# The last half piece of an expert's second weights: loaded a step ahead into a place of its own and copied by ScalarE

## The chip, the core and the metric

The kernel runs on one core of a Trainium2 chip. The metric is the device time of one execution in microseconds. Three runs of the kernel before gave 1069.84, 1070.74 and 1071.74 us; the median is 1070.74 us.

## What is computed

The input is a graph of 625 nodes with 768 features and 20,000 edges. A two-layer graph attention network is added to the normalised nodes, then a transformer block of one layer (causal attention with 12 heads and a mixture of 8 experts) is added to the result. The change touches only the mixture, which in the reference is:

```python
h2 = _ln(x, ln2_g, ln2_b).reshape(-1, d)          # 625 x 768
w, sel = jax.lax.top_k(h2 @ Wg, 1)                 # one expert per row
w = jax.nn.softmax(w, axis=-1)                     # of one value: 1
combine = zeros((n, 8)).at[arange(n)[:, None], sel].add(w)
hid = jax.nn.relu(jnp.einsum('nd,edf->enf', h2, W1) + b1[:, None, :])   # 3072 hidden
y = jnp.einsum('enf,efd->end', hid, W2) + b2[:, None, :]
moe = jnp.einsum('ne,end->nd', combine, y)
```

Each row needs only the expert that its gate chose. The weights of one expert are W1 (768 x 3072) and W2 (3072 x 768) in float32, 18.9 MB together.

## The kernel before

The graph layers and the attention fill the first 620 us or so and are not touched. The mixture works on rows sorted by expert in DRAM (`xg` holds the normalised rows, `xr` the sums so far with the row's number). Rows of one expert are cut into blocks of 128, 64 or 32 rows. A first block of 128 rows, of the expert that most rows of the first tile chose, is worked on ahead of the loop while the rest is still being sorted (`step_a`, line 1179). All other blocks are steps of one hardware loop (line 1333). A table made on the chip (lines 1264 to 1306) gives for every step its expert (row 0), whether this expert is new or the same as in the step before (row 1), the kind of the block (row 2) and its first row (row 3). In this input the loop has nine steps.

**The weights in SBUF.** There is one set of buffers for one expert: `w1[c]` and `w2[c]`, c = 0 to 2, each for 1024 of the 3072 hidden features. Each of the six pieces is loaded as two halves of 1536 KB (`load_piece`, lines 1028 to 1040; the issues are lines 1037 for W1 and 1031 for W2). The piece that this change is about is the second half of `w2[2]`, the last one in the order.

**A step** (`step`, line 1075) multiplies the block's rows with W1 in chunks (`into`, line 1091), copies the sums with VectorE (line 1095), turns them with TensorE (`turn`, line 1102), applies bias and ReLU with ScalarE (line 1107), and multiplies with W2 (`out_of`, line 1114) into `py`, which gathers over all chunks. In between it turns the next block's rows (`turn_rows`, lines 891 and 892). At its end VectorE adds `py` to the row sums (line 1166) and GpSimd scatters the rows to the output (line 1168). Blocks of 64 and 32 rows are laid side by side in the array, 2 or 4 at a time; there each `out_of` reads a whole `w2[c]`. The code of a step exists three times in the loop, one for each kind, behind `tc.If`.

**The order of the loads.** `load_expert(e, new)` (line 1066) comes after a step's own work (`all_of`, line 1325) and issues the loads for the *next* step: W1 in six halves, the bias row, W2 in six halves. SyncE issues them in exactly this order. Each waits until TensorE has read the buffer that it overwrites for the last time in this step, so the loads follow TensorE's reading through the step; the very last half can be issued only at the step's end. If the next step has the same expert, the issues are still executed by SyncE, with their waits, but move nothing (the condition `new`). `next_expert(i + 1)` (line 1319) reads the expert and the flag of the next step from the table into SyncE's registers at the start of a step.

Ahead of the loop the first expert's weights are loaded without a condition (lines 1051, 1052 and 1312), and one `load_expert` for the loop's step 0 follows `step_a` (line 1323). The loop is entered by every engine for itself: each adds an offset to the semaphores that it is responsible for, SyncE after it has read the number of steps (line 1331).

Of the kernel before, what the change touches and what calls it, by code (L numbers as in the profile page):

```python
# [9 lines left out]
F32 = mybir.dt.float32  # L10
F16 = mybir.dt.float16
BF16 = mybir.dt.bfloat16
I32 = mybir.dt.int32
# [11 lines left out]
D = 768  # L25
# [17 lines left out]
NS = E * 2 + N // B  # L43
# [4 lines left out]
FC = 1024  # L48
NFC = DF // FC
# [13 lines left out]
def gnn_moe_kernel(ctx: ExitStack, tc: tile.TileContext, p, out):  # L63
    nc = tc.nc
# [3 lines left out]
    keep = ctx.enter_context(tc.tile_pool(name="keep", bufs=1))  # L68
# [70 lines left out]
    def load_vector(b, v):  # L139
        nc.gpsimd.dma_start(b, row_bcast(v, D))  # L140
        return b[:R]
# [5 lines left out]
    with tc.tile_pool(name="gnn", bufs=1) as gp:  # L147
# [31 lines left out]
        with tc.tile_pool(name="oneh", bufs=12) as op_, \  # L179
# [20 lines left out]
            ahead = flat.bitcast(I32)[:G, GE:]  # L200
# [27 lines left out]
            def step(at, on_act):  # L228
                o = op_.tile([R, SH + 1], F16, name="step")
                if on_act:  # L230
                    nc.scalar.activation(o, iota[:, :SH + 1], AF.Sign, bias=at, scale=-1.0)  # L231
                else:
                    nc.vector.tensor_scalar(o, iota[:, :SH + 1], at, 2.0, op0=OP.is_lt, op1=OP.mult)
                return o
# [232 lines left out]

        sx = ctx.enter_context(tc.tile_pool(name="sx", bufs=1, side="right", reuse_waits="tile"))  # L470
        l1g = load_vector(sx.tile([B, D], F32, tag="xa", name="l1g"), p["L0_ffn_ln1_g"])
        l1b = load_vector(sx.tile([B, D + 1], F32, tag="ra", name="l1b")[:, :D], p["L0_ffn_ln1_b"])
        norms = keep.tile([R, T, 4], F32, name="norms")
        with tc.tile_pool(name="gw", bufs=2, reuse_waits="tile") as gw, \
# [68 lines left out]
            w2 = halves("w2", p["L0_gnn_W2"], KH, D)  # L543
# [138 lines left out]

    pos = [keep.tile([R, 1], I32, name=f"pos{t}") for t in range(T)]
    nblk = keep.tile([1, 1], I32, name="nblk")
    table = keep.tile([1, 4, NS + 1], I32, name="table")
    first = keep.tile([1, 1], I32, name="first")
    sxt = ctx.enter_context(tc.tile_pool(name="sxt", bufs=1, side="right", reuse_waits="tile"))
    xaT = sxt.tile([128, KD, B], F32, name="xaT")
    pool, SP, PE = mybir.EngineType.Pool, mybir.EngineType.SP, mybir.EngineType.PE
    rt = ctx.enter_context(ExitStack())  # L690
    ap = rt.enter_context(tc.tile_pool(name="rt", bufs=1, side="right", reuse_waits="tile"))
    with tc.tile_pool(name="att", bufs=1, reuse_waits="tile") as a1, \
# [107 lines left out]
        def queries_keys(j):  # L800

            i, c0 = j // 3, (j % 3) * 128
            qk[j] = [aw.tile([128, N], F32, name=n, bufs=2) for n in ("qT", "kT")]
            for dst, w, scale in ((qk[j][0], wq[i], D ** -0.5), (qk[j][1], wk[i], 1.0)):
                for a, b in ((0, SH), (SH, N)):
                    pp = ps.tile([128, 512], F32, tag="p1", name="pq")
                    for c in range(KD):
                        nc.tensor.matmul(pp[:, :b - a], w[:, c, c0:c0 + 128], hT[:, c, a:b],  # L808
                                         start=(c == 0), stop=(c == KD - 1))
                    nc.scalar.activation(dst[:, a:b], pp[:, :b - a], AF.Copy, scale=scale)  # L810
                    yield
# [172 lines left out]
        ahead = iter(())  # L984
        for i in range(len(units) + 2):
            if i < len(units):
                j, t = units[i]
                if t == 0:
                    for _ in ahead:
                        pass  # L990
                    ahead = queries_keys(j + 1) if j < last else iter(())
# [29 lines left out]
    W1, W2, b2 = p["L0_ffn_W1"], p["L0_ffn_W2"], p["L0_ffn_b2"]  # L1021
    w1, w2 = [None] * NFC, [None] * NFC

    def piece(ew, l, c):
        (w2 if l else w1)[c] = ew.tile([128, FC // 128, D] if l else [128, KD, FC], F32,
                                       name=f"ew{l}_{c}")

    def load_piece(e, l, c, **cond):
        if l:
            for k in range(0, FC // 128, 4):  # L1030
                nc.sync.dma_start(  # L1031
                    w2[c][:, k:k + 4, :],
                    W2[ds(e, 1), c * FC + k * 128:c * FC + (k + 4) * 128, :]
                    .rearrange("o (k p) d -> p (o k) d", p=128), **cond)
        else:
            for k in range(0, KD, 3):
                nc.sync.dma_start(
                    w1[c][:, k:k + 3, :],
                    W1[ds(e, 1), k * 128:(k + 3) * 128, c * FC:(c + 1) * FC]
                    .rearrange("o (k p) f -> p (o k) f", p=128), **cond)  # L1040

    def load_bias(e, **cond):
        nc.sync.dma_start(b2b, b2[ds(e, 1), :].to_broadcast([B, D]), **cond)
# [5 lines left out]
    piece(ewa, 0, 0)  # L1049
    piece(ewa, 1, 0)  # L1050
    load_piece(first_e, 0, 0)
    load_piece(first_e, 1, 0)
    b2b = mw.tile([B, D], F32, name="b2b", bufs=1)
    load_bias(first_e)

    def sums_so_far(row):
        rb = mw.tile([B, D + 1], F32, name="rb", bufs=1)
        nc.gpsimd.dma_start(rb, xr[ds(row, B), :])
        return rb

    def biases(e):
        bT = mw.tile([128, NK], F32, name="bT")
        of_e = bT_all.rearrange("p (e k) -> p e k", k=NK)[:, ds(e, 1), :]
        return bT, nc.vector.tensor_copy(bT, of_e.rearrange("p o k -> p (o k)"))

    def load_expert(e, new):

        with tc.manual_schedule(engines={SP}):
            for l in range(2):
                for c in range(NFC):  # L1070
                    load_piece(e, l, c, cond=new)
                if not l:
                    load_bias(e, cond=new)

    def step(M, xT, bT, rb, after=None):

# [120 lines left out]
    def row8(name, *shape, tag=None):  # L1197
        return ap.tile([1, *shape], F32, name=name, tag=tag or name)
# [67 lines left out]
    ioe = iota("ioe", [[0, NS], [1, E]], NS, E)  # L1266
    sel = row8("sel", NS, E)
    v.tensor_tensor(sel, inc[:, None, :].to_broadcast([1, NS, E]), ios, op=OP.is_le)
    tabf = row8("tabf", 4, NS + 1)
    v.memset(tabf, 0.0)  # L1270
    who = row8("who", NS)
    v.tensor_reduce(who, sel, AX.X, OP.add)
# [42 lines left out]
    row_0 = nc.values_load(table[0:1, 3, 0:1], engines=[pool], min_val=0, max_val=NR - B)  # L1315
    first_rows = nc.gpsimd.dma_start(xb, xg[ds(row_0, B), :])
    first_turned, = step_a

    def next_expert(i):
        return (nc.values_load(table[0:1, 0, ds(i, 1)], engines=[SP], min_val=0, max_val=E - 1),  # L1320
                nc.values_load(table[0:1, 1, ds(i, 1)], engines=[SP], min_val=0, max_val=1))

    load_expert(*next_expert(0))

    def all_of(step, e, new):
        with tc.manual_schedule(engines={PE}):
            for _ in step:
                pass
        load_expert(e, new)

    n_blk = nc.values_load(nblk[0:1, 0:1], min_val=1, max_val=NS)
    sp_order.close()
    with tc.For_i(0, n_blk, 1, iteration_sync="reg_based") as i:  # L1333
        e = nc.values_load(table[0:1, 0, ds(i, 1)], engines=[mybir.EngineType.DVE], min_val=0,
                           max_val=E - 1)
        kind = nc.values_load(table[0:1, 2, ds(i, 1)], min_val=0, max_val=2)
        row, row_next = (nc.values_load(table[0:1, 3, ds(k, 1)], engines=[pool], min_val=0,
                                        max_val=NR - B) for k in (i, i + 1))

        nc.gpsimd.dma_start(xb, xg[ds(row_next, B), :])  # L1340
        rb = sums_so_far(row)
        bT, s = biases(e)
        tc.add_manual_dep(s.ins, first_rows.ins.name, ORDER)

        then = next_expert(i + 1)
        with tc.If(kind == 0) as cmp:
            all_of(step(B, xbT, bT, rb, first_turned), *then)
        with cmp.Else():
            with tc.If(kind == 1) as cmp2:
                all_of(step(64, xbT, bT, rb, first_turned), *then)  # L1350
            with cmp2.Else():
                all_of(step(32, xbT, bT, rb, first_turned), *then)
# [31 lines left out]
```

## Time and profile before

| | us |
|---|---|
| median of 3 runs | 1070.74 |
| the profiled execution, its own time | 1070.6 |
| its span in the profile | 1067.9 |
| first block's work ahead of the loop | 627.9 to 698.8 |
| loop, TensorE from first to last matmul | 700.1 to 1055.2 |

The granted TensorE clock over the span is 0.985. In the page, engines are named PE (TensorE matmul), PEld (its weight loads), DVE (VectorE), ACT (ScalarE), POOL (GpSimd) and SP (SyncE); a "q" behind a name means the engine's instruction queue, so SPq L1031 is SyncE issuing the loads of line 1031. A group's line gives the engine, the operation, output and input, the count, then busy time and mean duration, then the engine's idle time just ahead of the group and what ended most of it. In the loop the steps begin, by TensorE's first matmul, at 700.13, 736.35, 801.68, 840.54, 866.12, 931.47, 965.72, 993.27 and 1027.52 us.

### The profile page before, as it was taken

How to read it: one execution, taken by the hardware profiler on the slowest of the kernel's cores; microseconds unless marked ns; L12 is line 12 of the kernel's file. 1: busy time of each engine (PE TensorE's matmuls, PEld its weight loads, DVE VectorE, ACT ScalarE, POOL GpSimd, SP SyncE). 2: the span in 40 equal slices, each digit the busy share in tenths (PEclk: the TensorE clock that was granted, in tenths of full speed). 3: DMA queues.
4: the chain of work that ended last, by engine and by line, in shares of the span. 5: the costliest groups of instructions: out<-in, count | busy, mean ns of one | idle time of the engine just before them, and what ended most of it. 6: DMA issues, size and time to landing. Idle time of an engine off the chain costs nothing. (4 is left out here: it accounts for less than half of the span.)

```text
span 1067.9 us, 14435 instructions
## 1 busy us (share of the span) xinstructions
PE 1006.7 (94%) x4763; PEld 574.8 (54%) x4764; DVE 451.7 (42%) x1264; ACT 319.0 (30%) x817; POOL 57.1 (5%) x97
## 2 busy tenths in 40 slices
PE   6889999999999999999999999999999889998993
PEld 4455465677656556666665654544453435533341
DVE  6886786484284910665438544011101121011211
ACT  6677553452231111444435211110202112021120
POOL 1200100000000100000001101000000000000000
PEclk9999999999999999999999999999999899998997
DMA  9300500301300347998002679012799948899693
GB/s 286 129 1 1 181 9 0 133 1 43 93 14 0 103 120 220 398 389 293 1 2 63 237 251 351 12 46 58 304 321 387 408 177 322 294 413 409 248 412 153
DMA packets 85669, 194.48 MB, mean 182 GB/s; under 512 B 32397, under 2 KB 34068, under 8 KB 85609
## 3 DMA queue, kind: packets, MB, share of 16 engines
q1 hardware_dynamic: 79817, 174.00, 44.3%
q0 software_dynamic: 5712, 19.54, 5.3%
q8 instruction: 36, 0.59, 0.2%
q10 hardware_dynamic: 80, 0.16, 0.1%
q14 instruction: 24, 0.20, 0.1%
HBM read 251.98 MB, written 38.37 MB: 272 GB/s over the span
## 5 line engine op out<-in xcount | busy, mean ns | idle before, releaser
L1114 PE MATMUL py<-ew,hbT 128*64 128x384 f32 (+2 forms) x960 | 196.0, 517 | 12.8 <-DMA ew<-in_L_ffn_W_dram 12.8
L1091 PE MATMUL ph<-ew,xbT 128*32 128x256 f32 (+2 forms) x864 | 153.9, 499 | 7.8 <-issue 4.5
L1114 PEld LDWEIGHTS py<-ew,hbT 128*64 128x64 f32 (+2 forms) x960 | 91.6, 149 | 97.7 <-issue 62.3
L1107 ACT ACTIVATE hbT<-tph,bT 128x64 f32<-128x64 f32 (+2 forms) x240 | 55.3, 333 | 264.2 <-PE tph L1102 162.3
L1091 PEld LDWEIGHTS ph<-ew,xbT 128*32 128x32 f32 (+2 forms) x864 | 63.9, 135 | 87.2 <-issue 79.9
L1166 DVE TENSOR_TENSOR yo<-yo,py 64x384 f32<-64x384 f32 (+2 forms) x40 | 23.0, 608 | 182.9 <-PE py L1114 182.5
L1095 DVE COPY hb<-ph 128x512 f32<-128x512 f32 (+1 forms) x39 | 24.5, 629 | 149.8 <-PE ph L1091 149.8
L528 PE MATMUL agg<-xl,zT 125*125 125x256 f32 (+1 forms) x300 | 79.8, 417 | 1.3 <-ACT zT L517 1.1
L528 PEld LDWEIGHTS agg<-xl,zT 125*125 125x125 f32 x300 | 54.5, 188 | 19.6 <-ACT zT L517 2.6
L231 ACT ACTIVATE step<-iota,past 125x314 f16<-125x314 f16 x120 | 55.9, 548 | 0.0
L356 PE MATMUL pp<-w,yT 128*125 128x512 f32 x120 | 55.3, 600 | 0.0
L628 PE MATMUL ph<-wr,h1T 128*125 128x384 f32 x160 | 52.8, 486 | 0.0
L590 PE MATMUL ph<-w,h1T 128*125 128x384 f32 x160 | 52.4, 486 | 0.0
L837 ACT ACTIVATE e<-e,nm 125x125 f32<-125x125 f32 (+4 forms) x60 | 36.0, 602 | 39.5 <-DVE nm L834 39.5
L248 PE MATMUL cps<-step,oh 125*125 125x314 f16 x181 | 37.4, 309 | 10.5 <-ACT step L231 5.4
L900 PE MATMUL po<-wpj,aT 128*125 128x384 f32 x120 | 44.3, 499 | 1.2 <-DVE nm L834 0.7
L241 DVE TENSOR_SCALAR oh<-iota,drel,upper 125x125 f16<-125x125 f16 x160 | 41.2, 317 | 3.4 <-PE cps L248 3.4
L166 PE MATMUL ph<-wr,yT 128*125 128x512 f32 x96 | 42.1, 593 | 0.1
L590 PEld LDWEIGHTS ph<-w,h1T 128*125 128x125 f32 x160 | 30.0, 188 | 21.2 <-issue 0.5
L628 PEld LDWEIGHTS ph<-wr,h1T 128*125 128x125 f32 x160 | 29.8, 187 | 20.8
L808 PE MATMUL pq<-hT,L_ffn_Wq 128*128 128x313 f32 (+1 forms) x144 | 40.9, 432 | 0.0
L834 DVE CUSTOM_DVE_ANT_0 e<-sc,later 125x125 f32<-125x125 f32 (+4 forms) x60 | 30.7, 544 | 24.1 <-PE sc L828 23.9
(328 smaller groups left out, 1248.9 us busy)
## 6 DMA issues: line engine op xcount, KB each, us to landing
ew<-in_L_ffn_W_dram SPq DMA_DIRECT2D x132, 1536.0 KB
xr<-zt SPq DMA_DIRECT2D x5, 3076.0 KB
xg<-zt SPq DMA_DIRECT2D x5, 3072.0 KB
w<-in_L_gnn_W_dram SPq DMA_DIRECT2D x4, 1536.0 KB
wr<-in_L_gnn_Wr_dram SPq DMA_DIRECT2D x4, 1536.0 KB
b2b<-in_L_ffn_b_dram SPq DMA_DIRECT2D x11, 384.0 KB
xb<-xg POOLq DMA_DIRECT2D x10, 384.0 KB, 6.1
rb<-xr POOLq DMA_DIRECT2D x9, 384.5 KB, 7.0
```

Of the source, the lines that this page charges most:

```text
L166: nc.tensor.matmul(pp[:R, :], yT[:, c, cols(t)], part(wr1, KD, c, i, 512), start=(c == 0), stop=(c == KD - 1))
L231: nc.scalar.activation(o, iota[:, :SH + 1], AF.Sign, bias=at, scale=-1.0)
L241: m = nc.vector.tensor_scalar(o, iota[:, :n], at, weight, op0=OP.is_equal, op1=OP.mult)
L356: nc.tensor.matmul(pp[:R, :], yT[:, c, cols(t)], part(w1, KD, c, i, 512), start=(c == 0), stop=(c == KD - 1))
L528: nc.tensor.matmul(self.agg[:R, c0:c0 + n], zT[:, s, :], xl[:, s, x0:x0 + n], start=(s == 0), stop=(s == T - 1))
L590: nc.tensor.matmul(ph[:R, :384], h1T[:, c, cols(t)], part(w2, KH, c, i, 384), start=(c == 0), stop=(c == KH - 1))
L628: nc.tensor.matmul(ph[:R, :384], h1T[:, k, cols(t)], part(wr2, KH, k, i, 384), start=(k == 0), stop=(k == KH - 1))
L808: nc.tensor.matmul(pp[:, :b - a], w[:, c, c0:c0 + 128], hT[:, c, a:b], start=(c == 0), stop=(c == KD - 1))
L900: mm = nc.tensor.matmul(pp[:R, i, :384], aT[:, c, cols(t)], wpj[i][:, c, :], start=(c == 0), stop=(c == KD - 1))
L1091: mm = nc.tensor.matmul(ph[g * M:(g + 1) * M, :C], xT[:, k, :M], w[:, k, o + g * C:o + (g + 1) * C], start=(k == 0), stop=(k == KD - 1))
L1107: nc.scalar.activation(hbT[c][:, k, r], tp[:, k, r], AF.Relu, bias=bT[:, f:f + 1])
L1114: mm = nc.tensor.matmul(py[g * M:(g + 1) * M, i, :384], hbT[c][:, k, g * M:(g + 1) * M], w[:, o + g * K + k, i * 384:(i + 1) * 384], start ...
```

## The change

The second half of `w2[2]` is no longer loaded into its place. A new buffer `ahead` (128 x 4 x 768 float32, 1536 KB) takes that half of an expert's W2. `load_expert` gets the expert and the flag of two steps: it issues the other 11 halves and the bias for the next step, then lets ScalarE copy `ahead` into the second half of `w2[2]`, and then issues the load of `ahead` for the step after the next, if that one has a new expert. The copy is made in every step. It reads what `ahead` holds, which is the half for the next step's expert (if the step after has the same expert, `ahead` keeps it). Ahead of the loop `ahead` is loaded once without a condition.

So that there is room for it, two pools on the right side of SBUF (`sx` and `sxt`, which hold the first block's rows) are closed once the first block has been emitted, and `ahead` is laid where they were. The table gets one more column, since the flag of step i + 2 is read. SyncE reads four table values for each step where it read two.

```diff
-        sx = ctx.enter_context(tc.tile_pool(name="sx", bufs=1, side="right", reuse_waits="tile"))
+        right = ctx.enter_context(ExitStack())
+        sx = right.enter_context(tc.tile_pool(name="sx", bufs=1, side="right", reuse_waits="tile"))
...
-    table = keep.tile([1, 4, NS + 1], I32, name="table")
+    table = keep.tile([1, 4, NS + 2], I32, name="table")
...
-    sxt = ctx.enter_context(tc.tile_pool(name="sxt", bufs=1, side="right", reuse_waits="tile"))
+    sxt = right.enter_context(tc.tile_pool(name="sxt", bufs=1, side="right", reuse_waits="tile"))
...
+    def load_half(to, e, c, k, **cond):
+        nc.sync.dma_start(to, W2[ds(e, 1), c * FC + k * 128:c * FC + (k + 4) * 128, :]
+                          .rearrange("o (k p) d -> p (o k) d", p=128), **cond)
+
     def load_piece(e, l, c, **cond):
         if l:
-            for k in range(0, FC // 128, 4):
-                nc.sync.dma_start(
-                    w2[c][:, k:k + 4, :],
-                    W2[ds(e, 1), c * FC + k * 128:c * FC + (k + 4) * 128, :]
-                    .rearrange("o (k p) d -> p (o k) d", p=128), **cond)
+
+            for k in range(0, FC // 128 - (4 if cond and c == NFC - 1 else 0), 4):
+                load_half(w2[c][:, k:k + 4, :], e, c, k, **cond)
...
-    def load_expert(e, new):
+    def load_expert(e, new, later_e, later_new):
+
 
         with tc.manual_schedule(engines={SP}):
             for l in range(2):
@@ -1071,6 +1075,8 @@
                     load_piece(e, l, c, cond=new)
                 if not l:
                     load_bias(e, cond=new)
+            nc.scalar.copy(w2[NFC - 1][:, FC // 128 - 4:, :], ahead)
+            load_half(ahead, later_e, NFC - 1, FC // 128 - 4, cond=later_new)
...
     first_turned, = step_a
+    right.close()
+    ahead = ctx.enter_context(tc.tile_pool(name="ahp", bufs=1, reuse_waits="tile")).tile(
+        [128, 4, D], F32, name="ahead")
...
-    load_expert(*next_expert(0))
-
-    def all_of(step, e, new):
+    of_0, of_1 = next_expert(0), next_expert(1)
+    with tc.manual_schedule(engines={SP}):
+        load_half(ahead, of_0[0], NFC - 1, FC // 128 - 4)
+    load_expert(*of_0, *of_1)
+
+    def all_of(step, *of):
         with tc.manual_schedule(engines={PE}):
             for _ in step:
                 pass
-        load_expert(e, new)
+        load_expert(*of)
...
-        then = next_expert(i + 1)
+        then = *next_expert(i + 1), *next_expert(i + 2)
```

More of the change, by code (lines that the diff above doesn't have):

```diff
@@ L1268, in gnn_moe_kernel @@
     v.tensor_tensor(sel, inc[:, None, :].to_broadcast([1, NS, E]), ios, op=OP.is_le)
-    tabf = row8("tabf", 4, NS + 1)
+    tabf = row8("tabf", 4, NS + 2)
     v.memset(tabf, 0.0)
```

## The prediction

> **What bounds the kernel now.** I read the page first. TensorE is busy 94% of the span, and only one group of it waits for transfers, the second weights (line 1114), for 12.8 us in all:
>
> ```profile
> L1114 PE MATMUL py<-ew,hbT 128*64 128x384 f32 (+2 forms) x960 | 196.0, 517 | 12.8 <-DMA ew<-in_L_ffn_W_dram 12.8
> ```
>
> Busy shares are averages, so I next took the stretches of 10 us from 570 us on (columns: TensorE, weight loads, VectorE, ScalarE, GpSimd busy; granted clock; DMA share; GB/s):
>
> ```profile
> 830.00:840.00 10.00, 6.00 (x36) 2.42 (x34) 2.22 (x5) 0.37 (x1) 0.93 (x1) 0.90 1.03 411
> ...
> 970.00:980.00 10.00, 9.09 (x118) 3.98 (x106) 2.14 (x5) 5.07 (x25) 1.10 (x2) 1.00 1.03 412
> 980.00:990.00 10.00, 6.60 (x34) 2.02 (x34) 0.22 (x1) 0.37 (x1) 0.00 (x0) 0.66 0.96 371
> ...
> 1040.00:1050.00 10.00, 6.30 (x34) 1.93 (x34) 1.09 (x2) 1.58 (x8) 0.00 (x0) 0.66 1.03 400
> ```
>
> The DMA engines are full at about 410 GB/s (a half piece of 1.57 MB each 3.85 us), TensorE has holes there, and its clock falls. The chain of waits says which transfer ends last:
>
> ```profile
> 841.44 20.14 DMA ew<-in_L_ffn_W_dram
> 861.58 0.14 issue
> 861.72 4.47 PE py L1114 x28
> ...
> 969.62 20.81 DMA ew<-in_L_ffn_W_dram
> ...
> 1031.82 20.44 DMA ew<-in_L_ffn_W_dram
> ```
>
> It is the last half of an expert's second weights, three times. TensorE's timeline places it (loop steps counted from 0; their shapes give 64, 128, 64, 32, 128, 64, 32, 64 and 32 rows). Steps 3, 6 and 8, of 32 rows, are too short for a load that began a step before:
>
> ```profile
> 858.13 0.84 PE L1114 MATMUL py<-ew,hbT 128*32 128x384 f32 x4
> 861.72 4.47 PE L1114 MATMUL py<-ew,hbT 128*32 128x384 f32 x28 [2.75 <-DMA ew<-in_L_ffn_W_dram]
> ...
> 982.70 5.33 PE L1114 MATMUL py<-ew,hbT 128*32 128x384 f32 x28 [3.10 <-DMA ew<-in_L_ffn_W_dram]
> 987.97 0.56 PE L891 MATMUL tpx<-ident,xb 128*128 128x128 f32 x2
> 988.46 0.84 PE L1114 MATMUL py<-ew,hbT 128*32 128x384 f32 x4
> 990.56 2.77 PE L1114 MATMUL py<-ew,hbT 128*32 128x384 f32 x28 [1.26 <-DMA ew<-in_L_ffn_W_dram]
> ```
>
> In step 3 one stall, in step 6 two (middle piece, then last); step 8 repeats step 6 at 1044.54 and 1052.39. After a stall the 28 matmuls take 4.47 or 5.33 us instead of 2.77: half clock.
>
> Last, the entry of the loop. SyncE's final (skipped) issue ahead of the loop and TensorE's first matmul in it:
>
> ```profile
> 698.82 0.07 SPq L1031 DMA_DIRECT2D ew<-in_L_ffn_W_dram  x1
> ...
> 700.13 4.08 PE L1091 MATMUL ph<-ew,xbT 128*64 128x512 f32 x18 [1.35 <-SPq L1333]
> ```
>
> TensorE waits there for SyncE, which sets up the loop's semaphores only after its last issue.
>
> **What the Trainium skill says.** "ScalarE: Activation LUTs" (What ACT_TABLE_LOAD costs) prices an activation with immediates at 186 ns and 0.833 ns per element. The trace shows copies of 512 and 1000 elements at 0.620 and 0.998 us, 0.77 ns apiece, so it agrees roughly; no run shows one of 3072. "TensorE: Matmul & The Clock Gate" (Part 1, What's actually happening) says that an idle window of about 3.4 us puts the array on half rate and a busy one brings it back. The trace agrees: the half-clock stretches it records are 6.83 us (838.08, 981.44, 1042.88) and 3.41 us (861.98), and the matmuls in them take twice as long. "Runtime: NRT & Kernel Launch" (Instruction fetch mechanics) says that a branch to instructions not yet held stalls for their fetch. TensorE's branch at 695.66 took 3.69 us, to 699.41; it lay under queued matmuls, and the change leaves it.
>
> **The change, part by part.** Times are of the profiled execution (span 1067.9 us, own time 1070.6 us, the 2.7 us between them around the span and unchanged; the median of the runs shown is 1070.74 us).
>
> *The copy.* 128x3072 elements: 0.186 + 3072 x 0.833 ns = 2.75 us (an estimate from the ScalarE page; 2.5 from the two copy rows; bounds 2.4 and 3.2). It starts when TensorE is done with the step. Its cover: ScalarE's next work, the turned hidden rows (line 1107), comes 5.9 us into a 32-row step and 10.9 us into the others, and the copy with about 1.3 us of branching ends at 4.2 us. Without that cover it would cost up to 2.75 us in each of 9 steps.
>
> *SyncE.* The half load into the extra place waits for the copy, and behind it on SyncE's queue stand the next step's table reads and all its loads. Two more table reads at 0.67 us each (a TENSOR_LOAD of 0.268 us and its register work) add 1.35 us a step. Per step the issues stay 12 halves and a bias; the half only changes place. Ahead of a 128-row step SyncE is late by about 0.5 us on a buffer freed 8 us into the step, and nothing waits for that. Ahead of steps 2, 5 and 7 it counts: there SyncE's issue opens the saturated stream.
>
> *The stream.* Before, after step 1, the last half for step 2 was issued at 801.88 and its bytes flowed from about 803.9. Now the extra half for step 3 goes in that slot, 2.85 us later (copy and hand-over); the stream of step 3 then needs 11 more halves instead of 12. So the last *loaded* half stands one place earlier, 3.9 us, but everything is later by a delay s. Of the 2.85 us, the output scatter (128 rows, 0.39 MB, issued 803.86) now fills about 0.9 in the gap: s = 2.0. Later no hole opens: from 806.7 the half and the two GpSimd row loads (0.79 MB) last 5.8 us, to 812.5; SyncE's next issue is at 804.75 + 0.37 + 3.8 + 1.35 = 810.2, plus some 2 us to flow (an issue into idle queues, 744.35, landed at 750.71: 6.36 less 3.85 gives 2.5). Bounds of s: 1.0 (more fill) and 2.9 (none). For step 8 the same working, with SyncE's first issue at 8.3 instead of 4.8 us into step 7 and the extra half flowing in an idle stretch, gives s = 2.2.
>
> *Step 3.* The final matmuls wait for the half before the last: 861.72 - 3.9 + 2.0 = 859.8, a stall of about 1 us, too short for the clock to fall (1.26 us at 989.3 left it full). With 2.8 us they end at 862.6 instead of 866.2: 3.6 us saved.
>
> *Steps 6 and 8.* The last stall goes, but the one for the middle piece is now next and is lengthened by s. From its end there remain 2.4 + 0.5 + 2.8 = 5.7 us at full clock, plus half of the time at half clock. That lasted 4.4, 3.7, 5.6 and 5.2 us in the four cases of before (from restart); I take their mean, 4.7: 5.7 + 2.35 = 8.05. Step 6: 982.70 + 2.0 + 8.05 = 992.75 against 993.34, 0.6 saved. Step 8: 1044.54 + 2.2 + 8.05 = 1054.8 against 1055.19, 0.4 saved. The phase of the clock's windows moves each by 0.9 either way.
>
> *Loop entry.* The same copy and skipped issue also stand ahead of the loop. TensorE finishes at 698.79; copy until 701.6; SyncE needs 1.2 us from its issue to the semaphore as before: TensorE starts at 703.0 instead of 700.13, 2.9 us lost. And TensorE is then idle for 4.2 us. On the 3.41 us grid of the recorded stretches a window ends at 701.55, idle for 2.8 us; the next has 1.5 us idle, and in step 6 one with 1.26 us idle did not restore the clock. So half clock until 708.4: 5.4 us, costing 2.7. Bounds: 0 (SyncE sets the semaphores without the copy) and 6. The first load of the extra place is in an idle stretch (670 to 700 us: 1 to 2 GB/s) and costs nothing; the end of the last step hides its copy under VectorE's 4 us of adds.
>
> *Sum.* + 2.9 + 2.7 - 3.6 - 0.6 - 0.4 = + 1.0 us: 1070.6 + 1.0 = **1071.6 us**, within 0.2% (2.1 us) of the time before, about what a measurement of this kernel can tell from no change.
>
> **The rivals.** *The entry is not paid* (faster): then only the gains stay, -4.6 us, 1066.0 us. For it: the profile shows that wait once, and 1.35 us only. Against it: the issue behind the copy is in SyncE's fixed order, and even skipped issues waited for their buffers (698.82). If only the clock holds, 1068.9.
>
> *The gap is not filled* (slower): s is 2.9 in all three streams, the last loaded half lands later, and each gain falls by 0.7 to 0.9: + 3.5 us, 1074.1 us. It decides from s = 2.4 on, where 1.0 + 3 x 0.4 passes 2.1 us. For it: at 802.3 to 803.9 DMA fell to 79 GB/s though the scatter was near. Against it: a scatter into idle queues (700.25) landed in 3 us.
>
> *The next step waits for the copy* (slower): its first matmul held for ScalarE's latest work, 9 x 2.85, 1096 us. Against it: step 2 began at 801.68 while VectorE's adds of step 1 still ran. *It does nothing*: with s at 3.9 the half before the last takes the stall over whole, gains gone, 1077 us.
>
> **How the numbers follow.** Forecast case 0.38; faster 0.34 (entry cheap or s near 1.0); slower 0.28 (gap 0.20, no gain 0.05, held step 0.03). Faster by over 0.2% 0.34, within 0.38, slower 0.28. The range, 1065.5 to 1075.0 us, takes in the first two rivals; the forecast case alone spans 1068.6 to 1072.9.
>
> **What would show it.** Right: the loop's first matmul near 703 with half clock behind it; in step 3 a stall of 1 us instead of 2.75; in steps 6 and 8 only the middle stall, some 2 us later in the step; a ScalarE copy of 2.75 us in each step. Wrong: TensorE in the loop by 701, or the middle stalls no later than before (both faster), or holes at the start of every step (slower).

## The result

The kernel after takes 1074.11 us (median of 13 runs, 1072.69 to 1078.31); the kernel before, on the same chip, 1070.74. The ratio is 1.0034, 95% interval 1.0019 to 1.0050: slower by 3.4 us, where I had forecast + 1.0. The time lies in the range, but outside the 1068.6 to 1072.9 us of the forecast case alone; it is near that of the rival "the gap is not filled" (1074.1). In two kernels further on, p1_four and p2_first, one execution was far longer than the others (5843.61 and 1094.32 us), and their ratios leave it out. The profiled execution of after has an own time of 1072.69 us, the lowest of its 13, and a span of 1069.3 us.

The page of after, the costliest groups. The second weights' wait has hardly shrunk (12.8 us before), and the copy is there at 2752 ns:

```profile
L1120 PE MATMUL py<-ew,hbT 128*64 128x384 f32 (+2 forms) x960 | 193.6, 507 | 12.0 <-DMA ew<-in_L_ffn_W_dram 12.0
...
L1078 ACT COPY ew<-ahead 128x3072 f32<-128x3072 f32 x10 | 27.5, 2752 | 43.9 <-PE py L1120 43.9
```

TensorE's timeline of after, its idle times from the loop's entry on:

```profile
703.71 11.83 PE L1097 MATMUL ph<-ew,xbT 128*64 128x512 f32 x48 [4.04 <-SPq L1345]
741.11 10.54 PE L1097 MATMUL ph<-ew,xbT 128*128 128x512 f32 x24 [1.78 <-DVE yo L1172]
845.29 7.56 PE L1097 MATMUL ph<-ew,xbT 128*32 128x256 f32 x96 [4.53 <-issue]
861.26 2.77 PE L1120 MATMUL py<-ew,hbT 128*32 128x384 f32 x28 [0.65 <-DMA ew<-in_L_ffn_W_dram]
865.17 2.79 PE L1120 MATMUL py<-ew,hbT 128*32 128x384 f32 x32 [0.77 <-DMA ew<-in_L_ffn_W_dram]
982.56 1.24 PE L1120 MATMUL py<-ew,hbT 128*32 128x384 f32 x4 [2.17 <-DMA ew<-in_L_ffn_W_dram]
986.49 4.34 PE L1120 MATMUL py<-ew,hbT 128*32 128x384 f32 x28 [2.69 <-DMA ew<-in_L_ffn_W_dram]
1041.96 5.43 PE L1120 MATMUL py<-ew,hbT 128*32 128x384 f32 x28 [4.24 <-DMA ew<-in_L_ffn_W_dram]
1049.78 2.77 PE L1120 MATMUL py<-ew,hbT 128*32 128x384 f32 x28 [0.65 <-DMA ew<-in_L_ffn_W_dram]
1053.70 2.79 PE L1120 MATMUL py<-ew,hbT 128*32 128x384 f32 x32 [0.78 <-DMA ew<-in_L_ffn_W_dram]
```

The entry is paid (4.04 us idle instead of 1.35). In step 3 two short stalls and full clock stand where 2.75 us and half clock stood. In step 6 the last stall is gone (no wait ahead of the x32 at 991). Step 8 has got worse: it waits 4.24 us for an earlier piece, and then twice more. The 4.53 us at step 3's start is TensorE's branch, which before had too (4.55); it is covered, because step 3 ends with a transfer. This pause comes and goes with kernels that have the same matmuls: before, after, e2_no_copy, e4_entry_act, r4_entry_only, s1_short, o1_order and p1_four have it (4.5 to 4.6 us), the other six start step 3 without it. So the waits of step 3 stand at other places in different kernels, and half clock with them; no run here separates that from the edits.

The chain of waits of after again shows a transfer in each of the three steps. In steps 3 and 8 it is now the half before the extra one; in step 6 it is the half ahead of that in the order, the second of `w2[1]` (landed at 986.35), while the half before the extra one landed at 990.27, 0.86 us before TensorE read it at 991.13:

```profile
844.49 20.55 DMA ew<-in_L_ffn_W_dram
...
966.01 20.34 DMA ew<-in_L_ffn_W_dram
...
1033.09 20.47 DMA ew<-in_L_ffn_W_dram
```

What the loop gains and loses is best read from one table for all kernels. For each stretch it gives, in us from the stretch's first matmul: SyncE's (or ScalarE's) load into ahead, its first load of w1, the landing of the last half that was loaded from memory in that stretch and that its last step needs, and the stretch's length. "Entry" runs from the end of the first block to step 2. All are read from the profiled executions.

```
kernel          entry   steps 2+3                 steps 5+6                 steps 7+8
                        ahead   w1  last  length  ahead   w1  last  length  ahead   w1  last  length
before          102.9      -   4.4  59.9   64.4      -   4.3  59.0   61.8      -   4.8  59.0   61.9
after           106.8    3.1   9.2  58.6   61.5    3.1   9.2  57.0   60.6    3.3   8.8  59.7   62.6
e1_entry        104.5    3.0   9.1  58.3   62.6    3.0   9.1  57.0   61.1    3.1   8.6  59.1   62.0
e2_no_copy      102.6   -4.4   2.9  54.8   58.7   -4.4   2.9  53.8   56.7    1.6   6.8  58.8   61.7
e3_act_queue    110.8    3.0   2.9  58.6   61.5    3.0   2.9  57.5   62.0    3.1   3.8  57.2   61.6
e4_entry_act    104.7    3.3   2.9  58.6   61.4    3.3   2.9  57.4   62.2    3.4   3.8  57.4   61.9
r1_reads        102.9      -   6.7  61.3   64.2      -   6.7  61.3   64.1      -   6.1  60.4   63.3
r2_late_reads   102.5    3.0   7.7  58.5   62.2    3.0   7.8  57.1   60.9    3.2   7.1  58.5   61.9
r3_split        102.5    1.8   6.2  57.6   61.5    1.8   6.1  56.8   60.8    2.1   6.0  57.9   61.8
o1_order        103.1    3.6   2.9  58.5   61.4    3.6   2.9  57.1   60.8    4.6   3.9  58.1   61.7
p1_four         102.4    1.0   7.1  56.7   59.6    1.0   7.7  56.6   61.4    2.1   7.3  58.6   62.4
p2_first        102.8    1.0   2.9  56.6   60.6    1.0   2.9  55.9   60.4    3.8   4.6  57.9   62.0
r4_entry_only   110.1      -   4.3  59.9   64.4      -   4.3  59.1   62.0      -   4.8  58.9   63.5
s1_short        104.6   -4.0   2.9  55.0   58.6   -4.0   2.9  53.9   56.7    1.6   6.8  57.5   62.5
```

The row of r4_entry_only tells how far one profile goes. Its loop is that of before, and its last halves land within 0.2 us of before's, but its steps 7 and 8 are 1.6 us longer. A half-clock stretch of 3.41 us costs about 1.7 us of matmuls (12.23 us for the first 24 of step 1 in r4_entry_only, 10.54 in before), and it need not stand at the same place twice. So the landings are the firm reading; a length can be off by about 1.7 us.

After against before: entry + 3.9, step 3 - 3.0, step 6 - 1.2, step 8 + 0.7, in all + 0.4. The own times of the two profiled executions differ by 2.1: 0.9 more is the first block ending later (699.66 against 698.78, in work that the change leaves alone; over all kernels here it ended between 698.8 and 700.3), 0.1 is after the last matmul, and 0.7 lies outside the span. The median stands another 1.4 above after's profiled execution.

### The profile page after: what moved, and what is told of

Read it like the earlier page. It is cut to its first block, busy times and chain, and to the rows that moved or that the text cites. A ratio compares the mean times of both kernels' runs of the same rounds, so it can differ in the third digit from the quotient of the medians.

```text
span 1069.3 us, 14527 instructions
## 1 busy us (share of the span) xinstructions
PE 1006.1 (94%) x4763; PEld 574.3 (54%) x4764; DVE 451.6 (42%) x1264; ACT 346.5 (32%) x827; POOL 57.1 (5%) x97
## 5 line engine op out<-in xcount | busy, mean ns | idle before, releaser
L1120 PE MATMUL py<-ew,hbT 128*64 128x384 f32 (+2 forms) x960 | 193.6, 507 | 12.0 <-DMA ew<-in_L_ffn_W_dram 12.0
L1113 ACT ACTIVATE hbT<-tph,bT 128x64 f32<-128x64 f32 (+2 forms) x240 | 55.3, 333 | 204.6 <-PE tph L1108 135.9
L1078 ACT COPY ew<-ahead 128x3072 f32<-128x3072 f32 x10 | 27.5, 2752 | 43.9 <-PE py L1120 43.9
```

The costliest lines, as they stand in the source:

```text
L1113: nc.scalar.activation(hbT[c][:, k, r], tp[:, k, r], AF.Relu, bias=bT[:, f:f + 1])
L1120: mm = nc.tensor.matmul(py[g * M:(g + 1) * M, i, :384], hbT[c][:, k, g * M:(g + 1) * M], w[:, o + g * K + k, i * 384:(i + 1) * 384], start ...
```

## The experiments

My theory after the result: the entry costs 4 us, and inside the loop each gain is cut because the stream of loads is opened later by the copy, and in step 7 also by the table reads. Rivals: the entry's cost is made up further on; the table reads cost nothing; or the DMA engines' rate alone sets the landings. Each ratio is to the kernel before, run on the same chip. The diffs are cut to the lines that matter, and the remarks behind # are not in the kernels.

**e1_entry: no copy ahead of the loop.**

```diff
-        load_half(ahead, of_0[0], NFC - 1, FC // 128 - 4)
-    load_expert(*of_0, *of_1)
+        load_half(ahead, of_1[0], NFC - 1, FC // 128 - 4)
+    load_expert(*of_0)        # loads all of w2, copies nothing
```

> The changed kernel without the copy ahead of the loop: step 0 gets its last half by a conditional load as in the kernel before, and the extra place is loaded once for step 1's expert. Everything inside the loop is as changed. Theory A (the entry is paid because SyncE's semaphore set-up stands behind the copy): TensorE enters the loop some 1.3 us after the first block instead of 4.0 and without a half-clock stretch, so 4 us less than the changed kernel: 1070.1 us, about 0.06% under the kernel before. Theory B (the loss lies in the loop or outside of the span): no more than 1 us less than changed, 1073 to 1074 us.

Measured: 1070.11 us, 0.9978 (0.9966 to 0.9990). Its median is 4.0 us under after's, which was not run beside it; by the ratios to before the two are 0.0056 apart, about 6 us. The loop's entry in the timeline of before, then of e1_entry:

```profile
700.13 10.52 PE L1091 MATMUL ph<-ew,xbT 128*64 128x512 f32 x48 [1.35 <-SPq L1333]
```

```profile
700.63 10.52 PE L1099 MATMUL ph<-ew,xbT 128*64 128x512 f32 x48 [1.01 <-SPq L1347]
```

The wait is back to 1.01 us, and the 48 matmuls take 10.52 us again, full clock. So the loop alone gains 1.1 to 3.6 us (the interval), not the 4.6 forecast, and in after the entry gives back more than that. (In this profile the entry's stretch is still 1.6 us longer than before's: a half-clock stretch stands at step 1's start, from 737.08 to 740.49. r2_late_reads and r3_split, with the same entry, have 102.5.)

**r4_entry_only: the entry alone.** The opposite edit: the copy and the skipped load ahead of the loop as in after; in the loop all is as in the kernel before (`then = next_expert(i + 1)`).

> The kernel before with the copy and the skipped load into ahead before the loop alone; inside the loop all is loaded as before, there is no copy and no further table read. Theory: the entry costs 4.0 us (2.7 of waiting and 1.3 of half clock in step 0's first products), and nothing else changes: 1074.7, 4.0 above the kernel before. Rival (what ends late at the entry is made up in steps 1 to 3, where TensorE waits for transfers that start by the clock of SyncE): 1 to 2 us above the kernel before, 1072.5; then the loop's part of the change costs the rest.

Measured: 1075.58 us, 1.0030 (1.0013 to 1.0047): + 3.9 by the medians, as the theory has it. The interval, 1.4 to 5.0 us, does not by itself shut out the rival's 1 to 2; the table speaks against it, since steps 2 and 3 take 64.4 us as before and nothing is made up there. Its profiled execution was a long one (own time 1079.42 us), and its timeline shows why an entry has no single price:

```profile
702.96 13.44 PE L1099 MATMUL ph<-ew,xbT 128*64 128x512 f32 x48 [3.77 <-SPq L1347]
742.28 12.23 PE L1099 MATMUL ph<-ew,xbT 128*128 128x512 f32 x24 [2.09 <-DVE yo L1174]
```

Here 3.77 us idle leave 2.9 us of half clock (13.44 - 10.52) in step 0 and 1.7 in step 1; in after 4.04 us idle left 1.3 (11.83 - 10.52). The granted clock shows where they part (the number behind GpSimd's), in after and then in r4_entry_only:

```profile
702.97:706.38 3.41, 2.67 (x8) 0.95 (x10) 0.00 (x0) 0.00 (x0) 1.09 (x2) 0.50 0.18 76
706.38:709.79 3.41, 3.41 (x19) 1.25 (x17) 0.00 (x0) 0.00 (x0) 0.04 (x1) 1.00 0.71 231
```

```profile
702.04:705.45 3.41, 2.49 (x6) 0.87 (x8) 0.00 (x0) 0.00 (x0) 0.65 (x2) 0.50 0.28 115
705.45:708.87 3.42, 3.42 (x10) 1.08 (x8) 0.00 (x0) 0.00 (x0) 0.48 (x1) 0.50 0.70 228
```

In after TensorE was idle for 0.74 us of the stretch in which it started again, and full clock followed; in r4_entry_only it was idle for 0.92 us, and half clock stayed for another 3.41 us.

**e2_no_copy: after without the copy** (so the last half of w2 is never refreshed).

```diff
-            nc.scalar.copy(w2[NFC - 1][:, FC // 128 - 4:, :], ahead)
```

> The changed kernel with ScalarE's copy left out: the extra half is loaded but the multiplication with the second weights uses what stands in the last half's place since the first block, so the rows of later experts are wrong there. Theory A (the copy costs by what waits for it on SyncE's queue): the entry is as before, the extra half is issued right behind the other eleven, s falls from 2.6, 2.0 and 4.7 us to about 0 to 1, and steps 3, 6 and 8 save about 5, 3 and 2 us: 10 us under the kernel before, 1060.5 us. Rival (the loads themselves, one half more in flight and two more table reads, are what costs): at most 4 us under the changed kernel, 1070 us.

Measured: 1060.61 us, 0.9894 (0.9868 to 0.9919). The total is as expected, the places are not: steps 3 and 6 gain 5.8 and 5.1 us against before, step 8 0.2. (Step 3 waits for no transfer here; its pause of 4.48 us at the start is no longer covered, so the earlier landing is not used in full.) The table shows that this run took away more than the copy's length: the load into ahead is issued 4.4 us before step 2 begins, since nothing reads ahead and the load waits for no step's end. In step 7 it moves nothing, because w1's first load still comes 6.8 us into the step, behind the two further table reads.

**e3_act_queue and e4_entry_act: the load into ahead on ScalarE.** Load and table reads of it move to ScalarE, in after (e3) and in e1_entry (e4), so that nothing on SyncE waits for the copy.

```diff
-            load_half(ahead, later_e, NFC - 1, FC // 128 - 4, cond=later_new)
+            load_half(ahead, later_e, NFC - 1, FC // 128 - 4, nc.scalar, cond=later_new)
-        then = *next_expert(i + 1), *next_expert(i + 2)
+        then = *next_expert(i + 1), *next_expert(i + 2, mybir.EngineType.Activation)
```

> The changed kernel with the extra half issued by ScalarE right behind its copy, and its two table reads made by ScalarE, so that SyncE's queue has neither. Theory A: at the entry TensorE still waits, now for ScalarE, about 1 us less than in the changed kernel; in step 7 SyncE's loads start at 4.8 us into the step instead of 8.8, so s of step 8 falls from 4.7 to about 2; steps 3 and 6 gain little, since nothing else is there to be sent in the gap after the copy: 3.5 us less than changed, 1070.6 us. Rival (SyncE's queue is not what matters, only that the half flows after the copy): within 1 us of changed, 1073 to 1075 us.

> Both of the two edits: no copy ahead of the loop, and the extra half issued by ScalarE. Theory A: the gains add up without the entry's share of the second: 4 + 2.6 us less than changed, 1067.5 us, 0.3% under the kernel before. Theory B: no better than the better of the two single edits.

Measured: e3 1077.26 us, 1.0045 (1.0030 to 1.0060); e4 1069.80 us, 0.9984 (0.9973 to 0.9995). Both are slower than my theories; e4 is what Theory B has, no better than e1_entry (1070.11). In e3 the entry got worse. Its timeline, ScalarE's queue and then SyncE's and TensorE's:

```profile
699.63 2.75 ACT L1078 COPY ew<-ahead 128x3072 f32<-128x3072 f32 x1 [4.79 <-PE py L1120]
702.52 0.12 ACTq L1030 DMA_DIRECT2D ahead<-in_L_ffn_W_dram  x1
```

```profile
702.73 0.50 SPq L1030 DMA_DIRECT2D ew<-in_L_ffn_W_dram  x2
```

```profile
704.52 7.70 PE L1097 MATMUL ph<-ew,xbT 128*64 128x512 f32 x24 [4.93 <-SPq L1345]
```

SyncE's own skipped load stands at 702.73, right behind ScalarE's at 702.52: in the trace it waits on a semaphore that ScalarE's load has been given as well, so SyncE waits for the copy all the same. TensorE's idle time is 0.9 us longer than in after, and half clock costs 2.3 us in step 0 (12.85 us for the 48 matmuls) and 1.7 in step 1, so that the entry is 4.0 us longer. In the loop the row of e4 is the useful one: w1's first load is issued at 2.9 us instead of 9.1, and the last landing of step 3 doesn't move (58.6 against 58.3). What is queued on SyncE behind the copy is thus *not* what holds steps 3 and 6. In step 8 it is: 59.1 to 57.4; but the stretch is only 0.1 us shorter, since the 28 matmuls behind its long stall ran at half clock (5.21 us), those behind e1_entry's stall of 1.61 us at full clock (2.77).

**r1_reads: the two table reads alone**, in the kernel before (`then, _ = next_expert(i + 1), next_expert(i + 2)`).

> The kernel before with the two more table reads in each step and nothing else of the change. Theory (w1's loads of the short step 7 stand behind everything that SyncE does at a step's end, so each read ahead of them counts there): the first load of w1 in step 7 is issued 1.3 us later than before (6.1 us into the step instead of 4.8), the last half piece lands as much later, and step 8 is longer by 1.3 us; steps 3 and 6 by 0 to 1.3 each; in all 1.3 to 3 us over the kernel before, most likely 1073. Rival (the transfers of a step are held by the rate of the DMA engines alone, and there is slack ahead of them): within 0.5 us of the kernel before.

Measured: 1077.54 us (6 runs), 1.0052 (1.0035 to 1.0069): + 5.8, more than any of my cases. Reads of the table on every queue, r1_reads in step 5 (name and times in ns, shortest, median, longest):

```profile
L1320 SPq TENSOR_LOAD <-table x2: 266/478/690, 933.9 to 935.3; - x2
...
L1321 SPq TENSOR_LOAD <-table x2: 275/584/892, 934.6 to 936.3; - x2
```

The two further reads took 0.69 and 0.89 us there, not 0.27, so w1's first load was 2.4 us later instead of 1.35 (also in step 2; 1.3 in step 7), and the last halves landed 1.4, 2.3 and 1.4 us later than before. (The stretches show 3.4 us of the 5.8: step 3 ended at full clock this time.) A read this long turns up now and then in other kernels too (0.80 us in step 2 of after, 1.11 in step 1 of p1_four, the longest); in the loop always 1 to 5 us after a load was issued, and why is open.

**r2_late_reads: e1_entry with the reads just ahead of the load into ahead**, behind the loads of w1 and w2.

```diff
-        then = *next_expert(i + 1), *next_expert(i + 2)
+        then = *next_expert(i + 1), i + 2
+            later_e, later_new = next_expert(later)   # in load_expert, behind the copy
```

> As e1_entry, but SyncE makes the two more table reads just ahead of the load into ahead, behind the loads of w1 and w2 of the next step. Theory: the reads stand under SyncE's wait for the copy and no longer ahead of w1's loads: step 8 is 1.3 us shorter than in e1_entry, steps 3 and 6 by 0 to 0.7: 1068.5 us, 1.6 under e1_entry. The reads now stand between the step's end and the load into ahead only if SyncE has no time for them earlier, which it has. Rival (step 8's loss is the copy and the hole behind the extra half piece, the reads cost nothing): 1070.1, as e1_entry.

Measured: 1069.62 us, 0.9986 (0.9973 to 0.9999): no different from e1_entry. The last landing comes 0.6 us earlier in step 8 and not earlier in steps 3 and 6. The stretch from the last matmul to the end grew from 12.8 to 15.2 us, 2.4 of it a pause of SyncE among its closing waits, without a releaser in the trace. If it stands in every execution, it hides as much of a gain, and the equal time proves nothing; the landings do. So the reads, costly by themselves, are almost free in after: they lie under the copy's wait and the 3.9 us in which the extra half flows.

**r3_split: r2_late_reads with half of the copy on GpSimd.**

```diff
-            nc.scalar.copy(w2[NFC - 1][:, FC // 128 - 4:, :], ahead)
+            nc.scalar.copy(w2[NFC - 1][:, FC // 128 - 4:FC // 128 - 2, :], ahead[:, :2])
+            nc.gpsimd.tensor_copy(w2[NFC - 1][:, FC // 128 - 2:, :], ahead[:, 2:])  # ahead of the output scatter
```

> As r2_late_reads, and half of the copy is made by GpSimd at the same time as ScalarE makes the other half. ScalarE's half should take 0.19 + 1536 x 0.833 ns = 1.47 us, GpSimd's about 1.75 us (from its 0.71 us for 625 elements a partition). Theory (the copy delays the issue behind it, and the transfer, by its own length, and steps 3, 6 and 8 wait for what lands last): 1.0 us off each of the three, 3.0 in all: 1065.5. Rival (the transfers are late for the DMA engines' rate, whatever the copy takes): 1068.5, as r2_late_reads. If GpSimd is slower than 2.75 us, it is later than r2_late_reads.

Measured: 1069.06 us, 0.9977 (0.9967 to 0.9986); not told apart from r2_late_reads by time (it has the same pause at the end). The load into ahead comes 1.2 us earlier in steps 2 and 5, the last landings 0.9, 0.4 and 0.6 us earlier, the stretches are only 0.1 to 0.6 shorter: half clock behind the stalls takes the rest (4.57 to 4.80 us for the 28 matmuls).

**s1_short: e1_entry with 96 instead of 3072 elements copied**.

> As e1_entry, but ScalarE copies 96 elements a partition instead of 3072 (the rest of the half piece is not copied, so that part of the second weights is stale): the copy takes 0.27 us instead of 2.75, and SyncE's load into ahead still waits for the step's end. Theory (each us of the copy moves the whole stream of the next step, and steps 3, 6 and 8 wait for its last piece): 2.5 us off each of the three, 7.5 in all: 1062.6, nearly e2_no_copy's 1060.6. Rival (what e2_no_copy won came mostly from the load no longer waiting for the step's end at all; the copy's length is in part covered by the table reads and the load's own way to the buffer, as halving it in r3_split, which moved the three steps by 0.9 in all, suggests): 1.7 us off, 1068.4.

Measured: 1062.30 us, 0.9910 (0.9888 to 0.9933): the theory's number, for another reason than it gave. ScalarE's and SyncE's queues of s1_short ahead of step 2, which begins at 804.89:

```profile
800.64 0.27 ACT L1080 COPY ew<-ahead 128x96 f32<-128x96 f32 x1 [0.35 <-PE py L1122]
```

```profile
800.93 0.37 SPq L1030 DMA_DIRECT2D ahead<-in_L_ffn_W_dram  x1
```

The copy of one part starts 4.2 us *before* the step ends, when the matmuls of that part are done. So the run didn't keep the wait for the step's end, as I had said it would; it resembles e2_no_copy. It did show the cure: the whole copy waits for the last of four parts.

**o1_order: the load into ahead in the following step**, for that step's own next expert, between the first and second load of w1[0]. No further reads; nothing of SyncE waits for a copy at the step's end.

```diff
+                if k and not c and cond and not whole:       # in load_piece
+                    load_half(ahead, e, NFC - 1, FC // 128 - 4, **cond)
-                load_half(ahead, later_e, NFC - 1, FC // 128 - 4, cond=later_new)
-        then = *next_expert(i + 1), *next_expert(i + 2)
+        then = next_expert(i + 1)
```

> As e1_entry, but the load into ahead is issued in the following step, for the expert of the loads around it, between the first and the second load of w1[0]; so it needs no further table reads, SyncE waits for no copy at a step's end, and the copy (2.75 us) is over when the load's turn comes. Theory (a step's stream is late by copy and table reads, because w1's loads stand behind both): w1's first issue is 2.6 to 4.5 us into a step instead of 8.6 to 9.1; no hole in the stream of step 7, step 8 shorter by 2.0; steps 3 and 6 shorter by 0.4 to 1.0 each, since the number of pieces that must land stays the same: 1067.0, 3.1 under e1_entry and 4.6 under the kernel before. Rival (the stream's first piece, whichever it is, starts 2.6 to 3.0 us into the step in both kernels): 1069.5 to 1070.1, as e1_entry.

Measured: 1067.69 us, 0.9969 (0.9959 to 0.9980). Each against its own runs of before, the medians give 1.6 us over e1_entry, half of what was expected (the ratios 1.0, with intervals that overlap): step 8's last half lands 1.0 us earlier, those of steps 3 and 6 don't (58.5 and 57.1); there the rival was right, the stream opens at 2.9 us whichever piece is first. That step 3 is 1.2 us shorter is clock: 2.85 us from landing to end instead of 4.35. TensorE's pause at the step's start (4.63 us, absent in e1_entry) leaves two short stalls at its end (0.36 and 0.76 us) where e1_entry has one of 3.08 us and half clock behind it.

**p1_four and p2_first: the copy in four parts**, each behind its own matmuls; p1 in e1_entry, p2 with o1_order's place but as the first load of the step.

```diff
-                nc.scalar.copy(w2[NFC - 1][:, FC // 128 - 4:, :], ahead)
+                for k in order:      # 0, 1, 2, 3; after 32-row steps 0, 2, 1, 3
+                    nc.scalar.copy(w2[NFC - 1][:, FC // 128 - 4 + k, :], ahead[:, k, :])
```

> As e1_entry, but the copy is made in four pieces of 768 elements, in the order in which the step's last products set their part of the place free. A piece should take 0.186 + 768 x 0.833 ns = 0.83 us (s1_short's trace shows that a copy of one part starts 4 us before the step's end, when that part's products are done); behind the end of a step of 64 or 128 rows stands one piece, of 32 rows two. So the load into ahead is issued 1.1 us into steps 2 and 5 and 1.9 us into step 7, instead of 3.0. Theory (what the copy costs is the time by which it delays this issue behind the step's end): the last landing comes 1.9 us earlier in steps 3 and 6 and 1.1 in step 8, 4.9 in all, 1064.8. Rival (halving the copy in r3_split brought 0.9 in all for an issue 1.2 us earlier, since half clock took a part back): 0.75 in each step per us, less up to 1.7 for half clock: 1066.5 to 1068.

> As o1_order (the load into ahead in the following step, without further table reads), but as the first of its loads, ahead of w1[0], and with the copy in four pieces as in p1_four. Theory: the load into ahead is issued 1.1 us (1.9 in step 7) into the step, its 3.9 us of transfer fill the time until w1[0]'s first half is free and on its way, and the stream has no hole: last landings 1.9 us earlier than in o1_order in steps 3 and 6, 1.0 in step 8: 4.8 under o1_order, 1063.0. Rival (w1[0]'s first half, which comes free 2.6 us into the step, starts the stream, and what goes before it brings little): 1066 to 1067.7.

Measured: p1 1067.32 us, 0.9968 (0.9956 to 0.9980); p2 1064.69 us (8 runs), 0.9939 (0.9917 to 0.9961), 6.3 under the kernel before and the fastest version here that leaves nothing out. p1 lies in its rival's range (1066.5 to 1068): against e1_entry the last halves land 1.6, 0.4 and 0.5 us earlier, where 1.9, 1.9 and 1.1 were expected. p2 lies between its theory (1063.0) and its rival. ScalarE's queue of p2_first ahead of step 2 (start 801.83), and SyncE's:

```profile
798.20 0.83 ACT L1083 COPY ew<-ahead 128x768 f32<-128x768 f32 x1 [0.97 <-PE py L1125]
799.42 0.83 ACT L1083 COPY ew<-ahead 128x768 f32<-128x768 f32 x1 [0.38 <-PE py L1125]
800.65 0.83 ACT L1083 COPY ew<-ahead 128x768 f32<-128x768 f32 x1 [0.40 <-PE py L1125]
802.00 0.83 ACT L1083 COPY ew<-ahead 128x768 f32<-128x768 f32 x1 [0.51 <-PE py L1125]
```

```profile
802.85 0.38 SPq L1030 DMA_DIRECT2D ahead<-in_L_ffn_W_dram  x1
804.70 5.52 SPq L1040 DMA_DIRECT2D ew<-in_L_ffn_W_dram  x3
```

Three parts lie under the step's last matmuls; the load is issued 1.0 us into the step instead of 3.0, and w1 follows at 2.9. Last landings against o1_order: 2.0, 1.2 and 0.2 us earlier (expected 1.9, 1.9, 1.0). Step 7 falls short because SyncE itself comes to the load only 3.8 us into it, behind its table reads.

## Why the prediction was right and wrong

**The invariant behind it.** In steps 2 and 3, from the issue that opens the stream (ahead or w1, whichever is first) to the last landing, the traces give 55.2 to 55.8 us in the nine kernels that send 12 halves and open the stream within the step (after, e1, e3, e4, r2, r3, o1, p1, p2), and 59.7 in before, with 13 (opened by its last half at 0.2 us). The difference, about 4, is one half. It holds only where no hole follows the first load: r1_reads, with 13 halves and w1 2.3 us later, needs 61.1, and e2_no_copy and s1_short, which open the stream 4 us before the step and send w1 7 us later, need 59.2 and 59.0. In steps 5 and 6 the nine spread more, from 53.9 to 55.6 (p1_four, with 6.7 us between ahead and w1), against 58.8 in before. So the step "the last loaded half stands one place earlier, 3.9 us, but everything is later by a delay s" was right, and s is the delay of the opening.

**The entry: mechanism right, mis-sized in the profile.** Idle 4.04 against 1.35 us, 2.7 for the forecast 2.9. For the clock I had 2.7 and after's profile shows 1.3, since a window with 0.74 us of idle in it already brought full clock back at 706.4, where I had half clock until 708.4. The profile's + 4.0 stands against the forecast + 5.6. Over runs the entry is + 3.9 by r4_entry_only's medians (1.4 to 5.0), and after less e1_entry, which were not run side by side, is 4.0 by the medians and 6.0 by the ratios: a spread that holds 5.6 too.

**s in step 3: 2.6, forecast 2.0.** The last loaded half landed 1.3 us earlier (59.9 to 58.6) instead of 1.9. The step that failed is "the output scatter now fills about 0.9 in the gap": the opening came 2.9 us later, and 0.3 of that was filled. Step 3 gained 3.0, not 3.6, and its stall was split in two, 0.65 and 0.77.

**s in step 6: 2.0, as forecast.** It gained 1.2 for 0.6, because half clock ended sooner (4.34 us for the 28 matmuls, and full clock behind them): by luck, within the 0.9 that the prediction allowed for the phase of the windows.

**s in step 8: 4.6, forecast 2.2.** This is the step that failed. "The same working" was wrong there: in step 7 nothing flows before SyncE's first load, so the extra half opens nothing that the others can follow at once, and the 11 halves behind it start with w1's first load. I had that at 8.3 us; it was 8.8, against 4.8 before. Counted as above, from the opening issue to the last landing, 12 halves take 54.0 to 54.3 us in steps 7 and 8 of before, r1, r4, e3, e4, o1 and p2, where the first two loads follow each other within 0.8 us, and 55.3 to 56.5 in after, e1, r2, r3 and p1, where w1 comes 3.9 to 5.6 us behind ahead. After opened its stream 1.5 us earlier than before and took 2.3 us longer for it. The stretches of step 7 (busy times of the engines, granted clock, DMA share, GB/s) show the dip between the extra half and w1 in after, and no dip in before:

```profile
1000.00:1003.00 3.00, 3.00 (x18) 0.99 (x16) 0.38 (x1) 0.00 (x0) 1.09 (x2) 1.00 1.01 406
1003.00:1006.00 3.00, 3.00 (x18) 1.10 (x16) 0.69 (x1) 0.79 (x4) 0.00 (x0) 1.00 0.86 264
```

```profile
1003.00:1006.00 3.00, 3.00 (x16) 1.05 (x14) 0.69 (x1) 1.45 (x8) 0.00 (x0) 1.00 1.02 421
```

Step 8 lost 0.7 instead of winning 0.4. e3_act_queue, with w1 at 3.8 us, landed the last half 2.5 us earlier than after, and e4_entry_act 1.7 earlier than e1_entry: it is w1's place behind copy and reads.

**The copy and its cover: right.** 2.752 us for the estimate of 2.75, so the price in "ScalarE: Activation LUTs" (What ACT_TABLE_LOAD costs) holds at 3072 elements a partition; no matmul of after waited for ScalarE, and "the next step waits for the copy" didn't happen. **The table reads:** 1.35 us was their price in quiet; r1_reads shows 2.4, yet in after they lie mostly under other waits.

**The sum.** Two small sums do not come out: the two copy rows (512 elements in 0.620 us, 1000 in 0.998) give 2.6 us for 3072, not 2.5, and "it does nothing", with the entry's + 5.6 alone, is 1076.2, not 1077. Neither moves the forecast. Right terms would have given + 3.9 - 3.0 - 1.2 + 0.7 = + 0.4 in the profiled execution, nearer to nothing than my + 1.0; the median says + 3.4. The loop part by itself is + 0.4 - 3.9 = - 3.5 in the profile, and over runs - 1.1 to - 3.6 (e1_entry). That the median meets the rival's 1074.1 is chance: the rival has s at 2.9 in all three streams, the runs show 2.6, 2.0 and 4.6, and its entry is the + 5.6. So some 2 us of the median are not placed: 0.9 is the first block's end, which scatters, and 0.7 lies outside the span. That the clock's phase at the entry differs from run to run would explain the median standing above the profiled execution (r4_entry_only's profile shows the entry 3.3 us dearer than after's), but I have a profile of one execution each and can't show it.

## What to carry to other kernels

Where a stream of loads is saturated, count the time from the issue that opens it and the number of pieces behind it: a piece taken out is worth one piece's time less the delay that its replacement puts on the opening, and where the queue has run empty, less the delay of the next issue too. A copy that frees a buffer should be cut as its readers are, so that only the last part stands behind them; that, a load order that needs no further reads, and no copy ahead of the loop, together turned + 3.4 us into - 6.3. Before adding a prologue that waits, count the clock behind the idle time it makes as a spread, not as a number.

## What the runs showed of the hardware that was not expected

- A read of four bytes of the table into SyncE's register took 0.26 to 0.34 us mostly; in the loop it took 0.36 to 1.11 us now and then, each time 1 to 5 us after that engine had issued a load. In r1_reads two such made 2.4 us of 1.35.
- GpSimd's copy of 128 x 1536 elements in float32 took 1.465 us, ScalarE's 1.472 us: no slower, for this form.

```profile
L1175 POOL COPY ew<-ahead 128x1536 f32<-128x1536 f32 x9 | 13.2, 1465 | 291.3 <-PE py L1122 291.3
```

- An idle time of 4.04 us cost 1.3 us of half clock in step 0 of one kernel, 3.77 us cost 2.9 in another. From 690 us to the last matmul the 14 traces hold 52 half-clock stretches, 20 of 3.41 us and 32 of 6.83; cut into pieces of 3.41 us, each piece with at most 0.74 us of TensorE idle in it was followed by full clock (52 pieces), each with 0.92 us or more by another piece of half clock (32).
- TensorE's pause of 4.5 us at step 3's start was there in eight kernels and absent in six that run the same matmuls (r1_reads lacks it and before has it).
- A load that is skipped still waits for its semaphores, those that another queue's load has been given too (e3_act_queue's entry, 4.93 us instead of 4.04).
